# Summing four scan directions in PSUM: the add to y moves from VectorE to TensorE and ScalarE

## The chip, the core and the metric

The kernel runs on one core of a Trainium2 chip. The metric is the time of one execution on the device in microseconds (us), the median of several runs. A core has five engines with instruction queues of their own, worked off in order: TensorE (PE in the profile; its weight loads are PEld), VectorE (DVE), ScalarE (ACT), GpSimd (POOL) and SyncE (SP), which here issues all DMA transfers. The engines wait for each other through semaphores. Products of TensorE land in PSUM, eight banks of 128 x 512 float32; everything else lives in SBUF or in DRAM.

## What is computed

Four images of 96 channels by 64 x 64 pixels pass through four layers. The first is a block with a selective scan over the 4096 pixels in four directions, followed by a gated normalisation and an MLP; the second is a smaller scan block; the third a Fourier block with an 8-bit feed-forward part; the fourth linear attention with such a part. The part that matters here is the scan of the first layer, for 192 channels, 16 states and 4 directions:

```
dt = softplus(einsum('bkrl,kdr->bkdl', dts_r, dt_projs_w) + dt_projs_b)
def step(hst, inp):
    dA  = exp(dt_t[..., None] * A[None])
    dBx = dt_t[..., None] * B_t * x_t[..., None]
    hst = hst * dA + dBx
    y_t = einsum('bkdn,bkn->bkd', hst, C_t)
ys = scan(step, 0, ...) + Ds * xs
ysum = y[:, 0] + undo_colmajor(y[:, 1]) + flipped(y[:, 2]) + undo_colmajor(flipped(y[:, 3]))
```

Directions 0 and 2 run along the rows of the image, forward and backward, directions 1 and 3 along its columns. The output is the sum over all four directions.

## The kernel before

**Stages.** `setup` and the first parts of `front` prepare the first image. Then `scan` runs over all four images; beside it a *stream* of other work (the rest of `front` for all images, the prepared weights, and `rest`, which is everything behind the scan of an image: `tail`, `l1`, `transform`, `middle`, `back`) is put between its instructions. When the scan is over, what is left of the stream runs alone: the end of the last image's `tail`, and its `l1` to `back`.

**The scan** walks 64 chunks: 4 images (batches) x 4 directions (order 0, 1, 3, 2) x 4 steps of 1024 pixels. A chunk has 24 tiles of 128 x 1024: 3 parts p of 64 channels, 4 groups g of states, 2 halves a; a tile holds 32 channels by 4 states. Each tile i goes through:

- `input_of` (L748): GpSimd makes w = u x B. It is issued 3 tiles ahead (`AHEAD`), into one of 9 buffers (`W`).
- `decay` (L144 by way of `act`): ScalarE makes h = exp(dt x A). It is issued two tiles ahead, and there are two buffers, in PSUM.
- the scan itself (L824): VectorE's TENSOR_TENSOR_SCAN over h and w.
- the product with C. Most tiles have it on VectorE (L832); for some GpSimd makes it (L844). `POOL_OUT` says for how many of 24, by image: 5, 8, 8, 8.
- a copy of the last column into `state`, for the next step of the direction: by ScalarE (L840) where VectorE makes the product, by GpSimd (L837) where GpSimd does. The last step of a direction has none.
- `sums` (L770): for each pair of tiles four products by TensorE, 32 columns wide each, add the 4 states of a channel and gather the 8 tiles of a part p in one PSUM bank, `py`. There is one such bank. They are issued three tiles behind the scan.
- `add_sums` (L782 or L785): when the bank holds a part's sums, VectorE adds them to `y`, which lies in SBUF and gathers all directions. In the column directions `y` is read and written with a step of 64 elements (L782), else plainly (L785). It is issued behind the scan of tile i, for a part that ended at tile i - 4. At the last direction the part of `y` then goes to DRAM (`y_ds`), and `y_there` lets the image's `tail` start on it.

**The order of the work** is written when the program is built, by a planner in the kernel. `tick` and `spend` add estimated costs to a clock per engine. After each scan and after each product `advance` compares: how late TensorE, ScalarE and GpSimd stand against VectorE's clock; if that is within a limit (`FIRST` = 2 us behind the scan, `SECOND` = 1 us behind the product), it lets the stream do one step. VectorE's own work for the stream is put off (`later`) until its inputs are estimated to be there (`flush`). `need` steps the stream by force until a chunk's inputs are made. SyncE's queue follows the same order.

```
late = max(chain["pe"] - 0.5, now["act"], now["pool"] - 6.0, now["pe"] - 2.0) - free
if not put_off and late <= slack:
    step()
```

**Constants** lie in SBUF for the whole kernel: `vec` (152 columns, 96 of them A), `negA`, `l1cen` and others. `ident`, a 128 x 128 identity, exists only in `setup`, where `idup` is made from it.

Of the kernel before, what the change touches and what calls it, by code (L numbers as in the profile page):

```python
# [26 lines left out]

DIRS = (0, 1, 3, 2)

POOL_OUT = (5, 8, 8, 8)  # L30

AHEAD, W = 3, 9

LANDED = 8.0

FIRST, SECOND = 2, 1
ENGINES = ("pe", "act", "dve", "pool")

_VECS = [
    ("g1", 1), ("b1", 1), ("bz01", 1), ("bz2", 1), ("cb01", 1), ("cb2", 1),
    ("dtb01", 4), ("dtb2", 4), ("A", 96),
    ("D01", 4), ("D2", 4), ("og01", 1), ("og2", 1), ("ob01", 1), ("ob2", 1), ("opb", 1), ("g2", 1), ("b2", 1),
    ("mb1", 3), ("mb2", 1),
    ("l1cb", 1), ("l1dtb", 2), ("l1A", 2), ("l1D", 2), ("l1og", 1), ("l1ob", 1), ("l1sc", 1),
# [10 lines left out]
def tile_hybrid(ctx: ExitStack, tc: tile.TileContext, I: dict, out: bass.AP):  # L57
# [65 lines left out]
    def right(name, bufs=1):  # L123
        return sb(name, bufs, "right")
# [7 lines left out]
    def act(o, i, func, own=False, **kw):  # L132

        if func in (AF.Exp, AF.Ln):
            if table[0] != "ln exp":
                nc.scalar.preload_act_table_set("natural_log_exp_and_others")  # L136
            table[0] = "ln exp"
        elif func in (AF.Silu, AF.Gelu, AF.Softplus):
            if table[0] != func:
                spend("act", 2.6)  # L140
            table[0] = func
        if not own:
            spend("act", 0.25 + size(o) * 0.86e-3, (i,), (o,))
        nc.scalar.activation(o, i, func, **kw)  # L144
# [76 lines left out]
    def cvec(shape, name):  # L221
        return const.tile(shape, F32, name=name)
# [10 lines left out]

    eps = cvec([128, 1], "eps")
    dve.memset(eps, EPS)

    idup = cvec([128, 32], "idup")
    cen = cvec([C, C], "cen")
# [3 lines left out]
    wz = cvec([C, DI], "wz")  # L242
    fold = cvec([128, 5], "fold")
    negA = cvec([128, 96], "negA")
    l1A = cvec([128, 2], "l1A")
    dsum = cvec([128, 3], "dsum")
    m1 = cvec([C, 384], "m1")
    l1cen = cvec([C, C], "l1cen")
    bn2 = cvec([C, 2], "bn2")
    wc_d = dram.tile([C + 1, 9, DI], F32, name="wc_d")  # L250
    l1wc_d = dram.tile([C, 9, C], F32, name="l1wc_d")
# [7 lines left out]
    def setup():  # L259

        held, (wk,) = pools(sb("set"))
        ident = wk.tile([128, 128], F32, name="ident")

        wraw = wk.tile([C, DI], F32, name="wraw")
        dma(wraw, I["w_inT"][:, 0:DI])
        bi = wk.tile([C + 1, DI], F32, name="bi")
        dma(bi[C : C + 1], I["bi"])
        cwr = wk.tile([C + 1, 9, DI], F32, name="cwr")
        dma(cwr, I["cwT"].partition_broadcast(C + 1))
        wx = wk.tile([C + 1, DI], F32, name="wx")  # L270
        pool.tensor_scalar(wx[rC], wraw, V("g1", rC), None, ALU.mult)
        pf = bank("pf")
        mm(pf[C : C + 1, 0:DI], lhsT=V("b1", rC), rhs=wraw, start=True, stop=True)
        dve.tensor_add(wx[C : C + 1], pf[C : C + 1, 0:DI], bi[C : C + 1])

        act(negA, V("A", n=96), AF.Exp)
        act(l1A, V("l1A", n=2), AF.Exp)
        dve.tensor_scalar_mul(negA, negA, -1.0)
        dve.tensor_scalar_mul(l1A, l1A, -1.0)
        dve.reduce_sum(dsum[:, 0:1], V("D01", n=4), axis=mybir.AxisListType.X)  # L280
        dve.reduce_sum(dsum[:, 1:2], V("D2", n=4), axis=mybir.AxisListType.X)
        dve.reduce_sum(dsum[rC, 2:3], V("l1D", rC, n=2), axis=mybir.AxisListType.X)

        def filters(wc):


            pool.tensor_mul(wc, wx[:, None, :].to_broadcast([C + 1, 9, DI]), cwr)
            dma(wc_d, wc)
            make_identity(nc, ident)
            dve.reduce_sum(idup, ident.rearrange("p (c n) -> p c n", n=4), axis=mybir.AxisListType.X)  # L290

        return held, filters

    def weights():
# [8 lines left out]
        def task():  # L303
# [32 lines left out]
            l1wc = wk.tile([C, 9, C], F32, name="l1wc")  # L336
            pool.tensor_mul(l1wc, w1raw[:, None, :].to_broadcast([C, 9, C]), l1cwr)
            dma(l1wc_d, l1wc)
            pool.tensor_scalar(l1cen, cen, dsum[rC, 2:3], None, ALU.mult)
            l1w = wk.tile([C, 2, C], F32, name="l1w")  # L340
            pw = bank("pw")
            for k in range(2):
# [315 lines left out]
    def scan(pls, advance, need, last_pass):  # L658
# [92 lines left out]
        def sums(i):  # L751

            ci, p, g, a = tiles[i]
            if a == 0:
                return
            if g == 0:
                py[ci, p] = ps.tile([128, 512], F32, tag="py", name="py")
            col = chunks[ci][1] % 2
            flags = dict(start=(g == 0), stop=(g == 3))
            for h in range(2):  # L760
                for e in range(2):
                    q = 32 * (2 * h + e)
                    o = py[ci, p][q : q + 32]
                    v = ws[i - 1 + e]
                    if col:
                        v = v.rearrange("p (w a q r) -> p q w a r", w=16, a=4, q=2)[:, h]
                        o = o.rearrange("p (w a r) -> p w a r", w=16, a=4)
                    else:
                        v = v[:, 512 * h : 512 * h + 512]
                    nc.tensor.matmul(o, lhsT=idup, rhs=v, **flags)  # L770
            t_sum[i - 1] = t_sum[i] = tick("pe", 1.5, t_out[i - 1], t_out[i])

        def add_sums(ci, p):
            b, k, step = chunks[ci]
            lo = start(ci)
            t = y[b][p]
            s = py.pop((ci, p))
            tick("dve", 0.7)
            if k % 2:
                w = lo // HH  # L780
                v = t.rearrange("p (a r w) -> p w a r", a=4, w=WW)[:, w : w + 16]
                dve.tensor_add(v, v, s.rearrange("p (w a r) -> p w a r", w=16, a=4))  # L782
            else:
                v = t[:, lo // 2 : lo // 2 + 512]
                dve.tensor_add(v, v, s)  # L785
                if k == DIRS[-1]:
                    for h, r in enumerate((lo64, hi64)):
                        dma(y_ds[b][64 * p : 64 * p + 64, lo + 512 * h : lo + 512 * h + 512], v[r])
                    if p == 2:
                        y_there.update((b, lo // 512 + h) for h in range(2))  # L790
# [14 lines left out]
        for i, (ci, p, g, a) in enumerate(tiles):  # L805
            b, k, step = chunks[ci]
            x = i % 24
            loads(ci, x)
            if x == 0:
                if step == 0:  # L810
                    states[b, k] = ck.tile([128, 24], F32, tag="state", name="state")
                if step == 0 and k == DIRS[-1]:
                    last_pass(b)
            if i >= 3:
                sums(i - 3)
            input_of(i + AHEAD)

            h, w = hs.pop(i), ws[i]
            pool_out = (x * POOL_OUT[b]) % 24 < POOL_OUT[b]
            o = w if pool_out else h  # L820
            r = slice(None, None, -1) if k >= 2 else slice(None)
            j = 4 * (2 * p + a) + g
            state = states[b, k][:, j : j + 1]
            dve.tensor_tensor_scan(o[:, r], h[:, r], w[:, r], state if step else 0.0, ALU.mult, ALU.add)  # L824
            t_out[i] = tick("dve", 2.35, t_h.pop(i), t_w.pop(i))
            if i >= 4 and tiles[i - 4][2:] == (3, 1):
                add_sums(*tiles[i - 4][0:2])
            flush(now["dve"])
            advance(now["dve"] + (0.0 if pool_out else 1.2), FIRST)
            cc = ccs[ci, g]  # L830
            if not pool_out:
                dve.tensor_mul(w, o, cc)  # L832
                t_out[i] = tick("dve", 1.23)
            if step < NCH - 1:
                last = 0 if k >= 2 else CH - 1
                if pool_out:
                    pool.tensor_copy(state, o[:, last : last + 1])  # L837
                    tick("pool", 0.19, t_out[i])
                else:
                    nc.scalar.copy(state, o[:, last : last + 1])  # L840
                    tick("act", 0.16, t_out[i])
            decay(i + 2)
            if pool_out:
                pool.tensor_mul(w, o, cc)  # L844
# [6 lines left out]
        add_sums(len(chunks) - 1, 2)  # L851

# [139 lines left out]
    def l1(b, stats, xa):  # L992
# [101 lines left out]
        yield from run([conv(m) for m in range(4)], n)  # L1094
        st2.close()

        st3, (ld, wk) = pools(right("l1m", two_groups(n)), right("l1n", n))
        carry = {}

        def states(k, m, order, w):  # L1100
# [528 lines left out]
def _layout(a):  # L1629
# [14 lines left out]
    db = p["dt_projs_b"].T  # L1644
    put("dtb01", db[0:128]); put("dtb2", db[128:192], both)

    put("A", p["A_logs"].reshape(4, 6, 32, 4, 4).transpose(2, 4, 0, 1, 3).reshape(128, 96))
# [22 lines left out]
    for e, rows in enumerate(((0, 6, 38), (32, 64, 80))):  # L1670
# [9 lines left out]
    wo = np.stack([wo[0:128], np.concatenate([wo[128:], wo[128:]])], axis=1)  # L1680
    wqkv = np.concatenate([np.asarray(a["L3_attn_Wqkv"]), np.asarray(a["L3_attn_bqkv"])[None]])
    d = dict(
        vec=vec, x=np.asarray(a["x"]).reshape(B, C, L),
        w_inT=p["in_proj_w"].T, bi=bi[None, 0:DI], cwT=p["conv_w"].reshape(DI, 9).T, xw=xw, dtw=dtw,
        out_projT=wo, mlp1T=p["mlp_w1"].T,
        mlp2T=p["mlp_w2"].T.reshape(3, 128, C).transpose(1, 0, 2),
# [30 lines left out]
```

## Time and profile before

| what | us |
|---|---|
| median of 3 runs | 6782.12 |
| lowest and highest run | 6772.63, 6800.76 |
| profiled execution | 6794.76 |
| its span | 6793.0 |
| first and last start of the scan (L824) | 97.9 and 6218.7 |
| granted TensorE clock, mean over the span | 0.746 |

The span begins with the first instruction and ends with the last; the profiled execution is 1.8 us longer than its span. A line of groups gives the source line, engine, operation, output <- inputs, shapes and count, then the busy time in us and the mean duration of one in ns, then the engine's idle time in front of these instructions and what ended most of it. A line of waits gives who waited <- for whom, the sum in us, how many times, and the longest. A line of windows gives a stretch, its length, and the busy time of each engine in it with the number of instructions, then the granted clock of TensorE (1 is full speed), the busy share of the DMA engines and GB/s. One float32 product of TensorE appears as two MATMUL records.

### The profile page before, as it was taken

Reading aid. Unit: us, or ns where it says so; the run is one execution under the profiler, and the core shown is the slowest. Engines: PE = TensorE matmul, PEld = TensorE weight load, DVE = VectorE, ACT = ScalarE, POOL = GpSimd, SP = SyncE. Lnnn points to the kernel's source line nnn. Section 1 sums busy time; section 2 is a strip of 40 time slices with the busy share of each in tenths; the row PEclk is TensorE's granted clock in tenths of the full one; section 3 lists DMA queues with packets and bytes.
Section 4 is the critical chain, followed back from the end, with each engine's and each line's share of the span. In section 5 each row is a group of like instructions: output and inputs, shape, how many; then the busy total and the mean of one; then the engine's idle time right before and its main releaser. Section 6 shows DMA issues by size and latency. Waiting matters only on the chain. (4 is left out here: it accounts for less than half of the span.)

```text
span 6793.0 us, 52666 instructions
## 1 busy us (share of the span) xinstructions
PE 4648.9 (68%) x15538; PEld 1509.5 (22%) x15538; DVE 5625.5 (83%) x3920; ACT 3691.3 (54%) x5194; POOL 5189.1 (76%) x2732
## 2 busy tenths in 40 slices
PE   6758667677677566656766676657676665567878
PEld 2112112121112124211111132211121242111354
DVE  3888779797789999998899998898899989985324
ACT  3556546565555554565555545565555455664335
POOL 4888879899769888898688788897797889983000
PEclk8767677686677778766777787668787777677887
DMA  4766666667534347445443365345443474442141
GB/s 147 212 193 192 190 180 198 194 208 223 166 109 151 114 132 259 149 130 160 145 147 111 122 225 184 126 142 154 142 134 122 146 250 136 140 153 91 43 113 50
DMA packets 502464, 1049.99 MB, mean 155 GB/s; under 512 B 138449, under 2 KB 252179, under 8 KB 501145
## 3 DMA queue, kind: packets, MB, share of 16 engines
q1 hardware_dynamic: 502176, 1046.63, 49.8%
q8 instruction: 123, 2.02, 0.1%
q14 instruction: 165, 1.34, 0.1%
HBM read 831.15 MB, written 211.09 MB: 153 GB/s over the span
## 5 line engine op out<-in xcount | busy, mean ns | idle before, releaser
L748 POOL TENSOR_TENSOR w<-u,bb 128x1024 f32<-128x1024 f32 x1536 | 3588.8, 2360 | 169.9 <-PE py L770 110.9
L144 ACT ACTIVATE h<-dt,negA 128x1024 f32<-128x1024 f32 x1536 | 1706.6, 1117 | 795.8 <-DVE w L832 429.3
L824 DVE TENSOR_TENSOR_SCAN h<-h,state,w 128x1024 f32<-128x1024 f32 x804 | 1887.0, 2347 | 271.4 <-ACT h L144 201.2
L832 DVE TENSOR_TENSOR w<-h,cc 128x1024 f32<-128x1024 f32 x1072 | 1308.9, 1221 | 56.0 <-DMA cc<-bc_d 18.1
L770 PE MATMUL py<-w,idup 128*32 128x512 f32 x6144 | 1121.1, 802 | 246.6 <-POOL w L844 78.2
L844 POOL TENSOR_TENSOR w<-w,cc 128x1024 f32<-128x1024 f32 x464 | 1092.2, 2354 | 191.6 <-DVE w L824 161.5
L824 DVE TENSOR_TENSOR_SCAN w<-h,state,w 128x1024 f32<-128x1024 f32 x348 | 814.5, 2340 | 46.1 <-ACT h L144 28.7
L840 ACT COPY state<-h 128x1 f32<-128x1 f32 x804 | 127.5, 159 | 1279.8 <-DVE w L832 1279.0
L824 DVE TENSOR_TENSOR_SCAN h<-h,w 128x1024 f32<-128x1024 f32 x268 | 612.9, 2287 | 100.7 <-ACT h L144 69.0
L98 PE MATMUL pc<-xp 97*64 97x512 f32 (+1 forms) x1152 | 401.3, 612 | 12.6 <-DMA xp<-wc_d 7.2
L770 PEld LDWEIGHTS py<-w,idup 128*32 128x32 f32 x6144 | 164.4, 126 | 1059.1 <-issue 605.7
L837 POOL COPY state<-w 128x1 f32<-128x1 f32 x348 | 64.5, 185 | 360.6 <-DVE w L824 353.1
L111 POOL TENSOR_TENSOR u<-dt,xi 128x512 f32<-128x512 f32 x160 | 217.3, 1376 | 158.6 <-ACT dt L144 147.9
L824 DVE TENSOR_TENSOR_SCAN w<-h,w 128x1024 f32<-128x1024 f32 x116 | 264.3, 2279 | 72.2 <-ACT h L144 55.0
L98 PE MATMUL pc<-xp,wc 96*96 96x512 f32 x576 | 275.1, 631 | 25.6 <-ACT u L144 25.6
L98 PE MATMUL pd<-xd,dtw 6*64 6x512 f32 (+1 forms) x512 | 210.9, 979 | 92.3 <-ACT xd L148 57.9
L98 PE MATMUL pcen<-t,cen 96*96 96x512 f32 x192 | 139.3, 866 | 158.9 <-POOL t L1341 77.0
L144 ACT ACT_TABLE_LOAD x176 | 225.8, 1283 | 31.9 <-PE pd L98 18.2
L136 ACT ACT_TABLE_LOAD x174 | 223.2, 1283 | 3.8 <-PEq L1707 0.7
L98 PEld LDWEIGHTS pc<-xp 97*64 97x64 f32 (+1 forms) x1152 | 150.6, 168 | 270.8 <-issue 235.4
L98 PE MATMUL po<-hq,q 128*96 128x512 fp8e5 x192 | 86.7, 575 | 167.0 <-POOL hq L1326 132.0
L98 PE MATMUL px<-xi,xw 128*96 128x512 f32 (+1 forms) x192 | 140.4, 990 | 87.3 <-ACT xi L144 82.4
(245 smaller groups left out, 6309.6 us busy)
## 6 DMA issues: line engine op xcount, KB each, us to landing
u<-u_d SPq DMA_DIRECT2D x384, 512.0 KB
dt<-dt_d SPq DMA_DIRECT2D x384, 512.0 KB
bb<-bc_d SPq DMA_DIRECT2D x256, 512.0 KB
cc<-bc_d SPq DMA_DIRECT2D x256, 512.0 KB
dt_d<-dt SPq DMA_DIRECT2D x128, 256.0 KB
u_d<-u SPq DMA_DIRECT2D x128, 256.0 KB
f_d<-fo SPq DMA_DIRECT2D x64, 384.0 KB
a<-f_d SPq DMA_DIRECT2D x64, 384.0 KB
```

Source lines behind the costliest of these rows:

```text
L98: nc.tensor.matmul(o, lhsT=lhsT, rhs=rhs, **kw)
L111: aside(0.2 + size(o) * 2.1e-3, o, a, b).tensor_mul(o, a, b)
L136: nc.scalar.preload_act_table_set("natural_log_exp_and_others")
L144: nc.scalar.activation(o, i, func, **kw)
L748: pool.tensor_mul(w, us[ci, 2 * p + a], bbs[ci, g])
L770: nc.tensor.matmul(o, lhsT=idup, rhs=v, **flags)
L824: dve.tensor_tensor_scan(o[:, r], h[:, r], w[:, r], state if step else 0.0, ALU.mult, ALU.add)
L832: dve.tensor_mul(w, o, cc)
L837: pool.tensor_copy(state, o[:, last : last + 1])
L840: nc.scalar.copy(state, o[:, last : last + 1])
L844: pool.tensor_mul(w, o, cc)
```

## The change

The add to `y` becomes part of the sums: as the last product of a part, TensorE multiplies the old `y` by the identity, into the same bank (`of_sums` gives the bank and the piece of `y` in one layout). ScalarE then copies the bank to `y` (`keep_sums`). The copy is issued behind the decay of tile i + 2, where the add stood behind the scan of tile i. The planner is told 0.7 us more of TensorE, 0.65 us of ScalarE, and no longer 0.7 us of VectorE.

`POOL_OUT` becomes 4, 7, 7, 7, and the limits `FIRST` and `SECOND` become 3 and 1.5 us.

To make room, `ident` becomes a constant, A is loaded straight into `negA` and leaves `vec`, and `l1cen` goes to DRAM in `weights` and is loaded in `l1` for each image, at the start of the pools of its scans.

```diff
-POOL_OUT = (5, 8, 8, 8)
+POOL_OUT = (4, 7, 7, 7)
...
-FIRST, SECOND = 2, 1
+FIRST, SECOND = 3, 1.5
...
+    ident = cvec([128, 128], "ident")
...
+    dma(negA, I["A"])
...
-        act(negA, V("A", n=96), AF.Exp)
+        act(negA, negA, AF.Exp)
...
+            l1cen = wk.tile([C, C], F32, name="l1cen")
             pool.tensor_scalar(l1cen, cen, dsum[rC, 2:3], None, ALU.mult)
+            dma(l1cen_d, l1cen)
...
-            flags = dict(start=(g == 0), stop=(g == 3))
+            flags = dict(start=(g == 0), stop=False)
...
-            t_sum[i - 1] = t_sum[i] = tick("pe", 1.5, t_out[i - 1], t_out[i])
+            if g == 3:
+                o, v = of_sums(ci, p)
+                nc.tensor.matmul(o, lhsT=ident, rhs=v, start=False, stop=True)
+            t_sum[i - 1] = t_sum[i] = tick("pe", 1.5 + 0.7 * (g == 3), t_out[i - 1], t_out[i])
...
-        def add_sums(ci, p):
+        def of_sums(ci, p):
             b, k, step = chunks[ci]
             lo = start(ci)
-            t = y[b][p]
-            s = py.pop((ci, p))
-            tick("dve", 0.7)
+            t, o = y[b][p], py[ci, p]
             if k % 2:
                 w = lo // HH
                 v = t.rearrange("p (a r w) -> p w a r", a=4, w=WW)[:, w : w + 16]
-                dve.tensor_add(v, v, s.rearrange("p (w a r) -> p w a r", w=16, a=4))
-            else:
-                v = t[:, lo // 2 : lo // 2 + 512]
-                dve.tensor_add(v, v, s)
+                return o.rearrange("p (w a r) -> p w a r", w=16, a=4), v
+            return o, t[:, lo // 2 : lo // 2 + 512]
+
+        def keep_sums(ci, p):
+            b, k, step = chunks[ci]
+            lo = start(ci)
+            o, v = of_sums(ci, p)
+            py.pop((ci, p))
+            tick("act", 0.65, t_sum[24 * ci + 8 * p + 7])
+            nc.scalar.copy(v, o)
+            if k % 2 == 0:
                 if k == DIRS[-1]:
...
-            if i >= 4 and tiles[i - 4][2:] == (3, 1):
-                add_sums(*tiles[i - 4][0:2])
             flush(now["dve"])
...
             decay(i + 2)
+            if i >= 4 and tiles[i - 4][2:] == (3, 1):
+                keep_sums(*tiles[i - 4][0:2])
...
-        st3, (ld, wk) = pools(right("l1m", two_groups(n)), right("l1n", n))
+        st3, (wp2, ld, wk) = pools(right("l1c"), right("l1m", two_groups(n)), right("l1n", n))
+        l1cen = wp2.tile([C, C], F32, name="l1cen")
+        dma(l1cen, l1cen_d)
```

More of the change, by code (lines that the diff above doesn't have):

```diff
@@ L42 @@
     ("g1", 1), ("b1", 1), ("bz01", 1), ("bz2", 1), ("cb01", 1), ("cb2", 1),
-    ("dtb01", 4), ("dtb2", 4), ("A", 96),
+    ("dtb01", 4), ("dtb2", 4),
     ("D01", 4), ("D2", 4), ("og01", 1), ("og2", 1), ("ob01", 1), ("ob2", 1), ("opb", 1), ("g2", 1), ("b2", 1),
@@ L247, in tile_hybrid @@
     m1 = cvec([C, 384], "m1")
-    l1cen = cvec([C, C], "l1cen")
+    l1cen_d = dram.tile([C, C], F32, name="l1cen_d")
     bn2 = cvec([C, 2], "bn2")
@@ L261, in setup @@
         held, (wk,) = pools(sb("set"))
-        ident = wk.tile([128, 128], F32, name="ident")
         wraw = wk.tile([C, DI], F32, name="wraw")
@@ L850, in scan @@
             sums(len(tiles) + i)
-        add_sums(len(chunks) - 1, 2)
+        keep_sums(len(chunks) - 1, 2)
     x1_ds, t_ds = {}, {}
@@ L1645, in _layout @@
     put("dtb01", db[0:128]); put("dtb2", db[128:192], both)
-    put("A", p["A_logs"].reshape(4, 6, 32, 4, 4).transpose(2, 4, 0, 1, 3).reshape(128, 96))
+    A = p["A_logs"].reshape(4, 6, 32, 4, 4).transpose(2, 4, 0, 1, 3).reshape(128, 96)
     put("D01", p["Ds"].T[0:128]); put("D2", p["Ds"].T[128:192], both)
@@ L1682, in _layout @@
     d = dict(
-        vec=vec, x=np.asarray(a["x"]).reshape(B, C, L),
+        vec=vec, A=A, x=np.asarray(a["x"]).reshape(B, C, L),
         w_inT=p["in_proj_w"].T, bi=bi[None, 0:DI], cwT=p["conv_w"].reshape(DI, 9).T, xw=xw, dtw=dtw,
```

## The prediction, made before the changed kernel ran

> **What bounds the kernel now.** I read the page's busy line first, then busy time by window, then the waits of VectorE (DVE), ScalarE (ACT) and GpSimd (POOL), then the groups that the change touches. The lists of line L824 put the first scan at 97.9 us; VectorE ends its last scan-stage instruction, the add at L785, at 6224.3 us. So the span has three parts: 98 us of preparation, 6126 us of scan stage, 569 us after it.
>
> The page's busy line and costliest groups (count, then busy us and mean ns of one, then idle before):
>
> ```profile
> PE 4648.9 (68%) x15538; PEld 1509.5 (22%) x15538; DVE 5625.5 (83%) x3920; ACT 3691.3 (54%) x5194; POOL 5189.1 (76%) x2732
> ...
> L748 POOL TENSOR_TENSOR w<-u,bb 128x1024 f32<-128x1024 f32 x1536 | 3588.8, 2360 | 169.9 <-PE py L770 110.9
> L144 ACT ACTIVATE h<-dt,negA 128x1024 f32<-128x1024 f32 x1536 | 1706.6, 1117 | 795.8 <-DVE w L832 429.3
> ...
> L832 DVE TENSOR_TENSOR w<-h,cc 128x1024 f32<-128x1024 f32 x1072 | 1308.9, 1221 | 56.0 <-DMA cc<-bc_d 18.1
> ...
> L844 POOL TENSOR_TENSOR w<-w,cc 128x1024 f32<-128x1024 f32 x464 | 1092.2, 2354 | 191.6 <-DVE w L824 161.5
> ...
> L840 ACT COPY state<-h 128x1 f32<-128x1 f32 x804 | 127.5, 159 | 1279.8 <-DVE w L832 1279.0
> ```
>
> A product with C costs 1.22 us on VectorE and 2.35 on GpSimd, and ScalarE stands idle 1279 us before its small state copies, waiting for VectorE. Busy time in the scan stage alone (window, length, then PE, PEld, DVE, ACT, POOL), and in one late stretch:
>
> ```profile
> 98.00:6224.00 6126.00, 4162.01 (x13804) 1271.41 (x13804) 5433.70 (x3620) 3441.26 (x4762) 5171.66 (x2705) 0.74 0.52 162
> ...
> 2778.00:3161.00 383.00, 222.87 (x780) 65.64 (x779) 362.63 (x235) 242.03 (x349) 372.22 (x197) 0.71 0.45 145
> ```
>
> VectorE is busy 89% of the stage, GpSimd 84%, ScalarE 56%, TensorE 68% at a mean granted clock of 0.74. In most stretches VectorE is fullest; in the second one GpSimd is (97%). So the stage is VectorE's 5434 us plus 692 us of its idle time. What that idle time waited for (us, times, longest), from VectorE's waits in that window:
>
> ```profile
> DVE h L824 <- ACT h L144: 270.2, 140, 13.6
> DVE w L824 <- ACT h L144: 83.7, 16, 51.7
> DVE y L782 <- PE py L770: 68.0, 26, 6.7
> DVE y L785 <- PE py L770: 64.8, 16, 16.0
> DVE h L824 <- POOL w L748: 51.0, 38, 3.0
> DVE h L824 <- ACT state L840: 44.1, 25, 7.2
> ```
>
> The 51.7 us is the start, outside the stage. Left are 302 us for ScalarE's decay h, 133 us in which an add of the sums waited for TensorE, 56 us for GpSimd's w (5 of them at another row), 73 us for states.
>
> **The change, part by part.** Counts are from the built programs' instruction order.
>
> *Adds leave VectorE.* 192 adds go, 96 of each form:
>
> ```profile
> L782 DVE TENSOR_TENSOR y<-y,py 128x512 f32<-128x512 f32 x96 | 114.9, 1197 | 68.1 <-PE py L770 68.0
> L785 DVE TENSOR_TENSOR y<-y,py 128x512 f32<-128x512 f32 x96 | 64.6, 673 | 64.8 <-PE py L770 64.8
> ```
>
> That is 179.5 us busy. In the timeline an instruction starts some 0.08 us before the end of the one in front, so 164 us comes off the path: **-164**.
>
> *Products come to VectorE.* GpSimd took 5, 8, 8, 8 of 24 per chunk, now 4, 7, 7, 7: 64 products over 64 chunks. Start to start one costs 1.14 us: **+73**.
>
> *The wait for the sums moves.* The 133 us at the adds, in 42 waits, leave VectorE; ScalarE's copy has them now. It stands in ScalarE's queue behind the decay of tile i+2, so it is asked for one product (1.2 us) and one decay (1.1) later than the add was, and what follows it, a state copy that itself waits for VectorE's next product, is needed some 2.3 us after that; the identity product in front takes 1.2 of this back. Net 3.4 us of cover. In the timeline 39 of the 133 us lie beyond the first 3.4 us of their wait, so **-94**; the bounds are -133 and 0. Queued behind the waiting copy are the stream's activations, the next state copies and the next decay, for which the scan waits.
>
> *ScalarE's load.* The trace has no copy by ScalarE out of py; the nearest are its 128x512 copies from other PSUM banks, ca from pca at 0.58 us and yb from pcb at 0.61. 192 at 0.58 are 111 us, and 48 more state copies at 0.16 are 8: 56% busy becomes about 60%. It lies beside VectorE wherever ScalarE waits (the 1279 us); it costs where the decay is already late, which was so at 155 of 1536 scans, a tenth. So 12 us at the least, 119 if each delayed a scan. I take **+35**, nearer the low end, because the late tenth comes in bunches where the copies are late too. For the column directions (96 of the copies) the destination steps by 256 bytes; the VectorE add with those steps took 1.197 us where the plain one took 0.673. [...] No row here shows ScalarE writing so.
>
> *TensorE's load.* 192 identity products, 128 rows by 128 columns by 512. The nearest row, avg in the gated stage, took 39.6 us for 64 records, two to a product: 1.24 us each, 238 us together, 68% busy becomes 74%. It isn't the fullest engine, but the sums are made in its queue. It already waits for the add before it may write the bank again:
>
> ```profile
> 2027.56 0.67 DVE L785 TENSOR_TENSOR y<-y,py 128x512 f32<-128x512 f32 x1
> ...
> 2028.29 3.89 PE L770 MATMUL py<-w,idup 128*32 128x512 f32 x16 [6.21 <-DVE y L785]
> ```
>
> In the stage this cost it 144 us. With the copy 2.3 us later than the add, all that stands behind it (next sums, the stream's products) is held longer, and the w buffers come free later: GpSimd waits 111 us for them today. Nine buffers against three tiles ahead leave about two tiles, 7 us. It gets only work and holds, so no gain; at the most a tenth of them, as with the late decays, reaches VectorE: (238 + 192 x 2.3) / 10 = 68. **+20**, nearer 0, for the buffers.
>
> *GpSimd's load* falls by 64 x 2.354 + 48 x 0.185 = 160 us. VectorE waited 56 us for it, and in stretches like the second window it was the limit. Bounds 0 and -56; **-15**.
>
> *Wider limits* (2 to 3, 1 to 1.5 us of estimated lateness) let the stream be stepped sooner. In the built order the stream stands 0.5 to 2 chunks earlier: the tail of batch 1 starts in chunk 30.7, not 31.8. Behind the scan stage stands the same last tail task and the same rest, so the 569 us stay. With the old limits in the changed program the last tail would start in chunk 63.7, and more would be left behind. The tail of batch 2 now stands one task to a chunk, where two shared one (4590 to 4707 us, TensorE busy 88 of 117). VectorE is idle 77 us in the three such windows of the later batches; half of it is the gain's bound. Against that, a later ScalarE is accepted: 140 late decays by up to 1 us. Bounds -40 and +140; **-10**: the old lateness was paid in a tenth of the scans, the spreading is seen in the order.
>
> *Setup*: one more transfer for A, a smaller vec, l1cen through memory (one store, four loads, each hidden by the forward scan in front of its use): under 2 us, 0 taken.
>
> **Sum**: -164 + 73 - 94 + 35 + 20 - 15 - 10 = -155. The profiled execution took 6794.8 us (span 6793.0), 12.6 above the median of the runs, 6782.1. So 6640 on the profile's footing, **6627 us** on the median's.
>
> **Rivals.**
>
> *A: the freed time isn't used.* Up to 2012 us VectorE is busy 78 to 88% by the windows and waits for the stream (front parts, table loads). If the chains there, and in the tails, set the pace, the adds' time turns into more waiting for h. A third of the adds and all of the moved wait lost: -109 + 73 + 35 + 20 - 15 - 10 = -6, so with the rest of the terms within their bounds 6700 to 6800. For it: VectorE's idle time clusters there. Against it: the adds' waits were VectorE's own.
>
> *B: slower, by ScalarE's queue.* A copy whose sums are late stops every decay behind it, and two decays ahead is all the scan has. Price: the 133 us stay; the copies land on a late ScalarE at 0.6 us, 119 in all; later steps add 140 x 1 us. -164 + 73 + 119 + 140 = +168 without any other gain, 6950; the middle of it about 6860. It decides from the point where the added lateness is over the 91 us by which adds exceed products: about 150 copies of 192 paid in full. Against it: only a tenth of the scans found the decay late.
>
> *C: more than the sum.* VectorE and GpSimd both get shorter, so stretches that alternate between them lose both: all 133 of the wait, 56 of GpSimd's, 40 by spread tails, ScalarE at 12: -164 + 73 - 133 + 12 - 56 - 40 = -308, 6474; the middle about 6520.
>
> *D: it doesn't do what it says.* The built order has the adds gone, 1136 products on VectorE and 400 on GpSimd, so no.
>
> **Chances.** Forecast (6560 to 6700) 0.50; C 0.20; A (6700 to 6815) 0.18; B 0.12. Range 6520 to 6770: it leaves out half of C, a bit of A and B. About 0.5% (34 us) is what a measurement can tell from no change: faster 0.77, same 0.11, slower 0.12.
>
> **What would show it.** Right: scan stage near 5970 us; VectorE about 5340 busy in it; no VectorE wait for py; ScalarE's copy of y at 0.6 us, its waits for py under 60 us; VectorE's wait for h under 350; the part behind the stage at 569. Wrong: h waits above 430 (B), a copy in the column directions over 1 us, GpSimd waiting over 200 us for py, or the part behind the stage longer by a tail task.

## The result, and the profile after

The changed kernel takes 6878.8 us (median; 6878.06 to 6882.23), the kernel before 6782.1 beside it: a ratio of 1.0108, interval 1.0079 to 1.0136. It is slower, by 73 us; the prediction was 6627. TensorE's granted clock, 0.758 in the profiled execution for 0.746 before, isn't lower. The profiled execution has a span of 6880.4 us. In the page's busy line and groups the lines have moved: the scan is L837, the product with C L843, the sums L773; the identity product is L777 and ScalarE's copy L797.

```profile
PE 4871.1 (71%) x15922; PEld 1574.9 (23%) x15922; DVE 5547.5 (81%) x3792; ACT 3842.0 (56%) x5434; POOL 5038.4 (73%) x2620
...
L144 ACT ACTIVATE h<-dt,negA 128x1024 f32<-128x1024 f32 x1536 | 1712.2, 1118 | 640.2 <-DVE w L843 406.4
L843 DVE TENSOR_TENSOR w<-h,cc 128x1024 f32<-128x1024 f32 x1136 | 1388.4, 1222 | 79.2 <-DMA cc<-bc_d 2.5
L773 PE MATMUL py<-w,idup 128*32 128x512 f32 x6144 | 1097.7, 799 | 487.5 <-ACT y L797 353.3
...
L777 PE MATMUL py<-y,ident 128*128 128x512 f32 x384 | 325.7, 937 | 15.4 <-DMA y<-yin_d 15.4
```

VectorE has 78 us less to do (5547.5 for 5625.5) and GpSimd 151 us less, as the change intends; TensorE has 222 us more, and it stood idle 353 us before the sums for ScalarE's copy, where it had waited 144 for the adds. By window (length, then PE, PEld, DVE, ACT, POOL), the scan stage and the part behind it:

```profile
98.00:6297.00 6199.00, 4372.01 (x14180) 1334.34 (x14180) 5354.22 (x3491) 3590.07 (x5001) 5021.48 (x2594) 0.75 0.52 160
6297.00:6880.00 583.00, 455.13 (x1625) 225.07 (x1624) 189.33 (x290) 228.08 (x397) 1.56 (x8) 0.80 0.27 78
```

The stage before, cut by the same measure:

```profile
98.00:6221.00 6123.00, 4159.57 (x13793) 1271.05 (x13797) 5430.77 (x3616) 3441.26 (x4762) 5171.66 (x2705) 0.74 0.52 162
```

Here and below the stage runs from the start of the first scan to the end of the last. Before it was 6123 us with 572 behind it; it is now 6199 with 583, although VectorE is busy 77 us less in it. So VectorE stands idle longer. Its waits (us, times, longest; the 51.2 is the start, outside the stage):

```profile
DVE h L837 <- ACT h L144: 358.3, 153, 15.9
DVE h L837 <- ACT state L851: 151.0, 68, 15.4
DVE w L837 <- ACT h L144: 94.0, 23, 51.2
DVE w L837 <- ACT state L851: 59.9, 15, 9.8
...
DVE h L837 <- POOL w L751: 24.6, 14, 7.7
```

No row for `py` is left: the 133 us of waiting for the sums are gone. But in front of the scans VectorE now waits 612 us for ScalarE (the four rows together without the start), where it waited 375. One of these waits, in ScalarE's timeline (start, duration, then in brackets the idle time in front) and then VectorE's:

```profile
4554.01 1.12 ACT L144 ACTIVATE h<-dt,negA 128x1024 f32<-128x1024 f32 x1
4555.07 0.58 ACT L797 COPY y<-py 128x512 f32<-128x512 f32 x1
4555.66 1.28 ACT L144 ACT_TABLE_LOAD   x1
4561.84 0.69 ACT L144 ACTIVATE za<-pz,fold 128x512 f32<-128x512 f32 x1 [4.89 <-PE pz L98]
4563.55 0.69 ACT L144 ACTIVATE za<-pz,fold 128x512 f32<-128x512 f32 x1 [1.02 <-PE pz L98]
4565.46 0.69 ACT L144 ACTIVATE zb<-pz,fold 128x512 f32<-128x512 f32 x1 [1.23 <-PE pz L98]
4566.04 0.15 ACT L851 COPY state<-h 128x1 f32<-128x1 f32 x1
4566.21 1.28 ACT L136 ACT_TABLE_LOAD   x1
4567.51 1.12 ACT L144 ACTIVATE h<-dt,negA 128x1024 f32<-128x1024 f32 x1
```

```profile
4557.30 2.34 DVE L837 TENSOR_TENSOR_SCAN w<-h,state,w 128x1024 f32<-128x1024 f32 x1
4568.73 2.36 DVE L837 TENSOR_TENSOR_SCAN h<-h,state,w 128x1024 f32<-128x1024 f32 x1 [9.09 <-ACT h L144]
```

Between two decays stand, beside the copy of `y` and a state, three activations of the tail with their table loads. These take 4.6 us of the 12.4 between the decays; 7.1 is idle time in which ScalarE waits for TensorE's `pz`. TensorE itself had stood idle for 13.44 us, at the end for a transfer, `xh`, before it began these products at 4559.76. So the decay behind them is late by more than ScalarE's load would tell. Added over all rows, ScalarE waited for TensorE 548 us in the stage before and 691 in the stage after.

### The profile page after: what moved, and what is told of

It reads as the page before. It is cut to its first block, busy times and chain, and to the rows that moved or that the text cites. A ratio compares the mean times of both kernels' runs of the same rounds, so it can differ in the third digit from the quotient of the medians.

```text
span 6880.4 us, 54043 instructions
## 1 busy us (share of the span) xinstructions
PE 4871.1 (71%) x15922; PEld 1574.9 (23%) x15922; DVE 5547.5 (81%) x3792; ACT 3842.0 (56%) x5434; POOL 5038.4 (73%) x2620
## 5 line engine op out<-in xcount | busy, mean ns | idle before, releaser
L751 POOL TENSOR_TENSOR w<-u,bb 128x1024 f32<-128x1024 f32 x1536 | 3589.0, 2361 | 265.3 <-PE py L773 224.5
L837 DVE TENSOR_TENSOR_SCAN h<-h,state,w 128x1024 f32<-128x1024 f32 x852 | 1999.3, 2347 | 401.7 <-ACT h L144 273.5
L843 DVE TENSOR_TENSOR w<-h,cc 128x1024 f32<-128x1024 f32 x1136 | 1388.4, 1222 | 79.2 <-DMA cc<-bc_d 2.5
L773 PE MATMUL py<-w,idup 128*32 128x512 f32 x6144 | 1097.7, 799 | 487.5 <-ACT y L797 353.3
L857 POOL TENSOR_TENSOR w<-w,cc 128x1024 f32<-128x1024 f32 x400 | 942.3, 2356 | 183.1 <-DVE w L837 154.6
L837 DVE TENSOR_TENSOR_SCAN w<-h,state,w 128x1024 f32<-128x1024 f32 x300 | 702.2, 2341 | 80.1 <-ACT state L851 48.7
L837 DVE TENSOR_TENSOR_SCAN h<-h,w 128x1024 f32<-128x1024 f32 x284 | 649.4, 2287 | 141.6 <-ACT h L144 84.8
L773 PEld LDWEIGHTS py<-w,idup 128*32 128x32 f32 x6144 | 156.3, 125 | 1258.5 <-issue 605.0
L98 PE MATMUL pc<-xp 97*64 97x512 f32 (+1 forms) x1152 | 419.4, 639 | 7.7 <-ACT dt L144 7.7
L777 PE MATMUL py<-y,ident 128*128 128x512 f32 x384 | 325.7, 937 | 15.4 <-DMA y<-yin_d 15.4
L837 DVE TENSOR_TENSOR_SCAN w<-h,w 128x1024 f32<-128x1024 f32 x100 | 228.1, 2281 | 79.6 <-ACT h L144 68.4
L144 ACT ACTIVATE dt<-pd,vec 128x512 f32<-128x512 f32 (+1 forms) x256 | 162.8, 684 | 66.2 <-DMA dt_d<-dt 54.3
```

Of the source, the lines that this page charges most:

```text
L98: nc.tensor.matmul(o, lhsT=lhsT, rhs=rhs, **kw)
L751: pool.tensor_mul(w, us[ci, 2 * p + a], bbs[ci, g])
L777: nc.tensor.matmul(o, lhsT=ident, rhs=v, start=False, stop=True)
```

## The experiments

In all of them "limits" are `FIRST, SECOND`; waits are VectorE's for ScalarE's decays and states in front of the scans, in the stage. Stage, behind and waits come from one profiled execution of each run, the time in us is the median of all. Ratios are to the kernel before on the same chip; where I take the difference of two ratios, its uncertainty is the root of the sum of the squares of both half-widths, times 6805 us, the median of before in those runs.

| run | limits | POOL_OUT | sums | us | ratio [interval] | stage | behind | waits |
|---|---|---|---|---|---|---|---|---|
| before | 2, 1 | 5 8 8 8 | add | 6782.1 | 1 | 6123 | 572 | 375 |
| after | 3, 1.5 | 4 7 7 7 | moved | 6878.8 | 1.0108 [1.0079, 1.0136] | 6199 | 583 | 612 |
| e1 | 2, 1 | 4 7 7 7 | moved | 6823.5 | 1.0033 [1.0011, 1.0054] | 6045 | 675 | 462 |
| e2 | 3, 1.5 | 5 8 8 8 | add | 6909.8 | 1.0156 [1.0127, 1.0186] | 6222 | 572 | 495 |
| e3 | 2, 1 | 4 7 7 7 | add | 6866.4 | 1.0095 [1.0065, 1.0126] | 6203 | 581 | 352 |
| e4 | 3, 1.5 | 5 8 8 8 | moved | 6896.6 | 1.0140 [1.0112, 1.0168] | 6209 | 582 | 667 |
| e5 | 3, 1 | 4 7 7 7 | moved | 6876.5 | 1.0093 [1.0073, 1.0112] | 6191 | 583 | 585 |
| e6 | 2.5, 1 | 4 7 7 7 | moved | 6811.2 | 1.0004 [0.9990, 1.0019] | 6143 | 563 | 569 |
| e7 | 2, 1, from the third image 3, 1.5 | 4 7 7 7 | moved | 6843.9 | 1.0046 [1.0029, 1.0062] | 6153 | 591 | 549 |
| e8 | 3, 1.5 | 4 7 7 7 | VectorE copies | 6990.8 | 1.0280 [1.0235, 1.0326] | 6311 | 573 | 475 |
| e9 | 5, 3, both behind the decay | 4 7 7 7 | moved | 6835.0 | 1.0044 [1.0025, 1.0063] | 6118 | 605 | 523 |
| e10 | 2, 2.5 | 4 7 7 7 | moved | 6809.0 | 1.0011 [0.9990, 1.0033] | 6159 | 574 | 560 |
| e11 | 1.5, 3 | 4 7 7 7 | moved | 6803.2 | 0.9987 [0.9973, 1.0000] | 6132 | 582 | 561 |
| e12 | 2, 1, from the second image 1.5, 3.5 | 4 7 7 7 | moved | 6800.3 | 0.9991 [0.9974, 1.0008] | 6117 | 569 | 521 |
| e13 | 2, 1, from the second image 6, 4 behind the decay | 4 7 7 7 | moved | 6841.7 | 1.0051 [1.0031, 1.0070] | 6120 | 606 | 546 |
| e14 | 3, 1.5 | 4 7 7 7 | no copy | 6833.6 | 1.0043 [1.0027, 1.0060] | 6156 | 566 | 587 |
| e15 | 3, 1.5 | 4 7 7 7 | no copy, no identity product | 6817.8 | 1.0015 [1.0000, 1.0029] | 6153 | 565 | 600 |
| e16 | 2, 1 | 4 7 7 7 | no copy, no identity product | 6737.3 | 0.9905 [0.9881, 0.9929] | 5964 | 675 | 392 |
| e17 | 2, 1, planner told the old costs | 4 7 7 7 | moved | 6809.1 | 1.0005 [0.9989, 1.0020] | 6132 | 584 | 534 |
| e18 | 2, 1, planner told nothing of the sums | 4 7 7 7 | moved | 6803.9 | 0.9993 [0.9973, 1.0013] | 6081 | 607 | 488 |

Two theories stood at the start. In *Theory L* the wider limits are what costs: steps of the stream that are let through late stand in front of a decay. In *Theory Q* it is the moved sums: copies in ScalarE's queue, and the bank they hold.

### The parts alone (e1 to e4)

e1 is the changed kernel with the old limits, e2 the kernel before with the wide ones; e3 is the kernel before with the new `POOL_OUT`, e4 the changed one with the old.

```diff
e1  -FIRST, SECOND = 3, 1.5        +FIRST, SECOND = 2, 1
e2  -FIRST, SECOND = 2, 1          +FIRST, SECOND = 3, 1.5
e3  -POOL_OUT = (5, 8, 8, 8)       +POOL_OUT = (4, 7, 7, 7)
e4  -POOL_OUT = (4, 7, 7, 7)       +POOL_OUT = (5, 8, 8, 8)
```

> The changed kernel with the limits of before (2 and 1 us); everything else as changed. In the built order the stream then stands later, and three tail tasks of the last image are left behind the scan stage instead of one. Theory L (the wider limits let the stream's activations in ahead of the decays, and that is what makes VectorE wait for ScalarE): the scan stage falls from 6205 us to about 5980, VectorE's waits for ScalarE (h and state together) from 612 back to about 400 us; with some 120 us of tail work more behind the stage the total is about 6680. Theory Q (the copies themselves, standing in ScalarE's queue and holding the only bank of the sums, are what costs): the scan stage stays within 40 us of 6205, waits for ScalarE stay above 550, total 6900 to 7000.

> The kernel before with the wider limits alone (3 and 1.5 us). In the built order as much is left behind the scan stage as before. Theory L: slower by about as much as the changed kernel's added waits, 6860 to 6930, VectorE's waits for ScalarE up from 375 to 500 or more. Theory Q: within 30 us of before, 6750 to 6810, waits for ScalarE near 375.

> The kernel before with 4, 7, 7, 7 products on GpSimd alone: 64 products more on VectorE. If VectorE's own work sets the pace of the scan stage (as the prediction's sum had it): 73 us slower, about 6850. If its waits set the pace and work put on it only fills idle time: within 25 us of before, 6760 to 6805. If GpSimd was the tighter one: faster by up to 56 us, 6730.

> The changed kernel with 5, 8, 8, 8 products on GpSimd as before: 64 products fewer on VectorE. If VectorE's own work sets the pace: 73 us faster than the changed kernel, about 6806. If its waits for ScalarE set the pace: within 25 us of the changed kernel, 6855 to 6905.

Alone, the wide limits make the kernel before 106 us slower (86 to 127), more than the whole change (33 us more than after, 5 to 61). VectorE's waits in e2 rise to 495 us while those for the sums stay:

```profile
DVE h L824 <- ACT h L144: 327.6, 135, 13.5
DVE w L824 <- ACT h L144: 77.5, 12, 51.5
DVE w L824 <- ACT state L840: 73.6, 21, 13.1
DVE y L782 <- PE py L770: 72.8, 29, 6.9
DVE h L824 <- ACT state L840: 68.2, 36, 13.1
DVE y L785 <- PE py L770: 63.3, 23, 11.7
```

One thing goes along with it. e2's stage by window has the work of before, but TensorE takes 57 us more for it (4217 for 4160):

```profile
98.00:6320.00 6222.00, 4217.47 (x13798) 1274.01 (x13798) 5441.44 (x3618) 3445.71 (x4762) 5171.48 (x2705) 0.72 0.51 160
```

Over whole executions the granted clock was 0.732 in e2 (mean of four) and 0.745 in the kernel before beside it. Among the 114 executions of the kernel before that were timed beside the experiments, the time is some 46 us longer for a clock lower by 0.01; by that slope, an estimate, up to 60 of the 106 us could come with the clock. Whether the lower clock is a cause of the longer time or comes of it, no run shows.

In the changed kernel they cost less, 51 us (27 to 75, after against e1), because there they also buy something. By window, e1's stage and what is behind it:

```profile
99.00:6144.00 6045.00, 4255.10 (x13962) 1301.92 (x13962) 5331.20 (x3446) 3521.94 (x4908) 5015.47 (x2593) 0.76 0.53 164
6144.00:6818.00 674.00, 554.14 (x1843) 255.63 (x1842) 221.77 (x335) 281.56 (x480) 1.56 (x8) 0.85 0.25 71
```

With the old limits the stage is 78 us shorter than before, but the last image's tail starts in chunk 63.7 and not 61.8, since the planner is told more of TensorE and ScalarE, and 103 us more is left behind the stage. The wide limits take 92 of these away (583 for 675) and lengthen the stage by 154. So Theory L holds for what happens in the stage, but e1 is no gain either: something else is missing. (The 6680 that Theory L gave for e1 was also added up wrongly: 98 of preparation, 5980 of stage, 583 and 120 behind it are 6781.) The products alone (e3) cost 65 us (44 to 86); undone in the changed kernel (e4) they bring nothing back, 22 us slower and not outside the uncertainty of 27.

### How wide, and where (e5 to e7, e9 to e13)

The edits of e7, e12 and e13 are given in words.

```diff
e5   +FIRST, SECOND = 3, 1          e6   +FIRST, SECOND = 2.5, 1
e10  +FIRST, SECOND = 2, 2.5        e11  +FIRST, SECOND = 1.5, 3
e7   +FIRST, SECOND = 2, 1 in images 0 and 1; 3, 1.5 in images 2 and 3
e12  +FIRST, SECOND = 2, 1 in image 0; 1.5, 3.5 in the others
e9   +FIRST, SECOND = 5, 3
     -            advance(now["dve"] + (0.0 if pool_out else 1.2), FIRST)
...
                  decay(i + 2)
     +            advance(now["dve"], FIRST)
e13  as e9 from the second image on, with 6, 4; the first as in e1
```

> The changed kernel with 3 us behind the scan and the old 1 us behind the product. What the first limit lets in stands in front of the next decay in ScalarE's queue, what the second lets in stands behind it. If the first limit is what makes decays late: VectorE's waits for ScalarE stay above 570 us (612 in the changed kernel), total 6860 to 6900. If the second is: they fall to about 480, the scan stage to about 6080, and with the same one tail task behind (583 us) the total is about 6760. If both share: about 6820.

> The changed kernel with 2.5 and 1 us. If the wait for ScalarE grows evenly with the limits: between the old limits (462 us of waits, stage 6045) and the wide ones (612, 6199), so about 520 and 6110. One or two tail tasks are left behind the stage in the built order, 583 to 640 us. Total 6800 to 6840. If only the last step from 2.5 to 3 costs: stage about 6060, total 6750.

> The changed kernel with the old limits for images 0 and 1 and the wide ones for images 2 and 3. If the price of the wide limits (154 us in the stage for four images) spreads over the images: stage about 6045 + 77 = 6120, with two tail tasks behind 625, total about 6845. If it is paid where many front parts are made, in image 0 alone: stage about 6050, total about 6775, less than before.

`FIRST` alone carries the price: with 3 and 1 the time is that of the changed kernel, with 2.5 and 1 it is back at before's. e7 lies between e1 and after: the two later images pay for their wide limits too (1550 and 1548 us of stage, against 1472 and 1515 in e1).

My arithmetic for this was a cover: the decay of tile i + 2 is wanted one scan and one product (3.6 us) after the product of tile i and takes 1.1, so stream work let through in front of it has some 2.4 us from the product's end; 2 lies below that and 3 above. A step behind the product has 3.6. From this came Theory C.

> The changed kernel with the stream's step behind the scan moved behind the decay of tile i + 2, and limits 5 and 3 there (both now stand behind the decay; in the built order the last tail begins in chunk 62.7, between the 61.2 of the changed kernel and the 63.7 of the one with the old limits). Theory C (cover): what costs is stream work on ScalarE in front of a decay that has only 2.4 us of cover from the end of the product, so out of its way VectorE's waits for ScalarE are at most the 462 us of the changed kernel with the old limits, the stage is near 6040, the part behind it 620 to 650, the time 6760 to 6800. Theory E (early): stream work costs wherever it is brought forward, by the same as with wider limits: waits about 600, stage 6190, time above 6880.

> The changed kernel with the limits 2 and 2.5: the old one behind the scan, a wide one behind the product. The last tail begins in chunk 61.3, as in the changed kernel (61.2). Theory C: the step behind the product has 3.6 us of cover, so 2.5 stays within it: waits for ScalarE 460 to 500 us, stage 6045 + 23 for two more tail tasks = about 6070, behind 585, time about 6750. Theory E: as the changed kernel, waits 600, stage 6190, time 6870.

> The changed kernel with the limits 1.5 and 3: tighter than the old one behind the scan, wider still behind the product; the last tail begins in chunk 61.2. Theory C: 3 is still within the 3.6 us of cover, and fewer steps stand in front of the decay: waits for ScalarE 430 to 480 us, stage about 6050, behind 583, time about 6730. Theory E: waits 600, stage 6190, time 6870.

Half of it held. The stream stands in the same place as after (the last tail starts in chunk 61.3 and 61.2, after in 61.2), but bought behind the product it costs 66 to 82 us less: e10 and e11 are 0.0097 and 0.0121 below after in ratio. So the step in front of the decay is the dear one. e9 came out between the two theories, with 523 us of waits and a stage of 6118. But the gains forecast, to 6750 and 6730, didn't come: the stage is 87 to 114 us longer than e1's, about what the shorter part behind gives. In e11 and e9 the first image had by far the most of the waits (221 and 210 us, against 121 in e1; no later image more than 121), hence the next two.

> The changed kernel with the old limits (2, 1) in the first image and (1.5, 3.5) in the others; the last tail begins in chunk 61.8, as in the kernel before. Theory F (the remainder is the first image's): the first image as with the old limits throughout, 1521 us, the others as in the run with 1.5 and 3, 1520 + 1515 + 1497, so a stage of 6053, 590 behind it, time about 6740. Theory E (it is paid wherever the stream is early): the first image's gain is given back by the others, stage 6120 to 6140, time about 6800.

> The changed kernel with the old limits and places in the first image, and in the others both steps behind the decay with limits 6 and 4; the last tail begins in chunk 62.8, so about 35 us more than before is left behind the stage. Theory F: first image 1521, the others as in the run with both steps behind the decay, 1490 + 1505 + 1499, so a stage of 6015 to 6035, 620 behind it, time about 6750. Theory E: stage 6110 or more, time above 6820.

Theory F fell. The first image came as forecast, 1519 us in both, but the second, 1520 and 1490 in e11 and e9, came at 1555 and 1562: what the first image no longer paid, the second did. e11 and e12 tie with before; with e18 below (0.9987 to 0.9993) they are the best versions with the moved sums.

### The place without the limits (e17, e18)

The planner can also be led to the same place of the stream by what it is told of the sums, with the limits at 2 and 1. In e17 it is told what it was told before, in e18 nothing.

```diff
-            t_sum[i - 1] = t_sum[i] = tick("pe", 1.5 + 0.7 * (g == 3), t_out[i - 1], t_out[i])
+            t_sum[i - 1] = t_sum[i] = tick("pe", 1.5, t_out[i - 1], t_out[i])
...
-            tick("act", 0.65, t_sum[24 * ci + 8 * p + 7])
+            tick("dve", 0.7)        (e17; in e18 the line is gone)
```

> The changed kernel with the old limits 2 and 1, the planner told of the sums what it was told before (0.7 us of VectorE, nothing for the identity product and the copy); the last tail begins in chunk 61.2, as in the changed kernel. If the late steps are what costs (Theory L): stage 6045 + 23 = about 6070, behind 575, time about 6745. If the earlier position has the price itself (Theory E): stage 6130 to 6190, time 6805 to 6870.

> The changed kernel with the old limits, the planner told nothing of the sums; the last tail begins in chunk 63.0, between the 63.7 of the changed kernel with the old limits and the 61.8 of the kernel before. Theory L: stage about 6060, behind 620 to 640, time about 6790. Theory E: stage 6080 to 6100, behind the same, time about 6820.

e17's stage by window:

```profile
98.00:6231.00 6133.00, 4316.12 (x14180) 1316.52 (x14180) 5359.91 (x3492) 3585.64 (x5001) 5019.49 (x2594) 0.76 0.52 162
```

The same instructions as after in another order (PE, ACT and DVE counts agree but for one of DVE), the last tail at the same 61.2, and yet 67 us less of stage: that is the price of the late steps. It includes whatever comes with the clock: TensorE is busy 56 us less for the same products (4316 for 4372), at a mean clock of 0.766 over all executions for after's 0.759. And 87 us more than e1: that is the price of the earlier stream itself, two tail tasks more in the stage, which give back 91 behind it. Put side by side, stage and rest behind it come to 6686 to 6733 us in e1, e6, e10 to e12, e17 and e18, and to 6695 before: wherever the stream stood, with limits up to 2.5 in front of the decay, the profiles gave one time within 0.7%.

### What the moved sums cost by themselves (e8, e14 to e16)

e8 keeps the identity product and lets VectorE copy the bank, in the add's old place. e14 leaves out ScalarE's copies, e15 and e16 leave out the identity products as well, so the directions aren't summed there; the planner is told the same costs, and the order of the rest is the same.

```diff
e8   -            nc.scalar.copy(v, o)
     +            dve.tensor_copy(v, o)        (behind the scan, VectorE told 0.7)
e14  -            nc.scalar.copy(v, o)
e15  as e14, and
     -                nc.tensor.matmul(o, lhsT=ident, rhs=v, start=False, stop=True)
     -            flags = dict(start=(g == 0), stop=False)
     +            flags = dict(start=(g == 0), stop=(g == 3))
e16  as e15, and  +FIRST, SECOND = 2, 1
```

> The changed kernel, but VectorE copies the bank of the sums to y, at the place where the add stood; ScalarE has no copies and the planner charges VectorE 0.7 us in their stead. If the 192 copies in ScalarE's queue add their part to the late decays: VectorE's waits for ScalarE fall from 612 to about 500 (495 with the wide limits alone), its waits for TensorE at the copy come back with 100 to 180 us, its busy time grows by 110 to 180; total 6880 to 6960. If the copies are harmless and TensorE's identity products and holds are the cost: waits for ScalarE stay above 580 and the total goes over 6980.

> The changed kernel without ScalarE's 192 copies of the bank to y; the sums over directions are left out of the output, the order of everything else is the same. My sum: the copies cost 35 us, so about 6845. Theory P (the price of the copies is what was freed): they hold ScalarE 154 us (192 at 0.80) and it waits 34 us in front of them, nearly all of it seen by the scan, so 6700 to 6730, VectorE's waits for ScalarE near 450. Theory A (the freed time isn't used, whoever makes the sums): less than 35 us, waits stay near 600.

> The same, and without the 192 identity products on TensorE (326 us busy in the changed kernel). My sum: another 20 us, so 6825. Theory P: GpSimd's waits for TensorE fall from 226 to about 110 us, another 20 to 60 us of time, so 6650 to 6700. Theory A: 6840 or more.

> The same with the old limits 2 and 1, to be held against the changed kernel with the old limits (6823). My sum: 55 us less, 6770. Theory P: VectorE's waits for ScalarE fall from 462 to about 330, the stage from 6045 to about 5900, time 6660 to 6690. Theory A: stage 6020 or more, time 6790 to 6820.

e8 is 117 us (80 to 154) slower than after: VectorE waits 217 us for `py` again. Of the two engines, ScalarE is the better one for the copy.

e14 and e15 weigh it: after against e14, the copies cost 44 us (22 to 67), e14 against e15, the identity products 19 (4 to 34); both together 87 (65 to 109) with the old limits (e1 against e16). That is my sum's size, 55, or somewhat more, and far less than Theory P asked for. The 19 is a net price: with the identity products gone the granted clock is lower, 0.740 for 0.762. In e15, free of everything that the moved sums put on ScalarE and TensorE, VectorE still waits as long for the decays (the scan is one line higher here):

```profile
DVE h L836 <- ACT h L144: 353.4, 146, 16.9
DVE h L836 <- ACT state L850: 153.7, 68, 15.2
DVE w L836 <- ACT h L144: 95.8, 14, 51.9
DVE w L836 <- ACT state L850: 48.5, 13, 9.6
```

Its stage by window:

```profile
98.00:6251.00 6153.00, 4208.75 (x13798) 1279.25 (x13798) 5368.59 (x3491) 3449.27 (x4810) 5014.65 (x2594) 0.73 0.52 161
```

The waits are 600 us without the start, where e2, with the same limits and the adds, has 495. From e2 to e15 VectorE loses 73 us of work in the stage and 135 of waits for `py`, 208 together, and the stage gets 69 shorter; 105 came back in these rows. That is Theory A: half of the freed time turns into another wait. With the old limits the waits rise less, from 375 to 392 us, but more is left behind the stage. e16's two windows:

```profile
98.00:6063.00 5965.00, 4047.90 (x13580) 1239.64 (x13580) 5327.14 (x3447) 3382.31 (x4718) 5012.34 (x2594) 0.74 0.53 166
6063.00:6737.00 674.00, 558.63 (x1841) 255.99 (x1840) 221.09 (x334) 281.11 (x479) 1.56 (x8) 0.83 0.25 71
```

The stage is 159 us shorter than before and 103 more is left behind. By the 87 us that the two tail tasks cost inside the stage (e17 against e1), some 72 of the 159 would be left with the stream in its place of before, an estimate. Free sums over directions would bring 65 us (48 to 81) all told; the moved sums cost 87.

## Why the prediction was wrong

From before to after by way of e16 and e1: the gains -65, the copies and identity products +87, the wide limits +51; together +73, which is the result. The sum had -200 (adds, products, the wait, GpSimd), +55 and -10. So of the 228 us between the forecast of -155 and the result, 135 lie in the gains, 61 in the limits and 32 in the copies and identity products. Two steps failed.

- **The larger: the gains, -200, taken as time off the stage because VectorE no longer works or waits there.** Its parts hold by themselves. The waits for `py` are gone (133 us, predicted 94 net), and ScalarE waits 34 us for the sums, as against the 39 that I left it. Products and GpSimd's relief, +58, measured +65 (e3). An add took less of the path than I said: counted in the trace of before, where an add stands alone between scan and product (91 of 192), a plain one moves the product by 0.44 us and one with steps by 0.93, so 132 us for all and not 164. But the gains together came to 65 us (e16). With the wide limits, 208 us less of work and waits made the stage 69 shorter, and 105 came back as waits for ScalarE (e2 to e15): the scan can't start earlier than its decay, and with the adds gone the decays are what it finds late. Rival A said this and priced it at 6700 to 6815; e11, e12 and e18, the best versions with the moved sums, lie there, at 0.9987 to 0.9993 of before. The changed kernel itself lies above it, by the limits.
- **The other: "Wider limits ... -10: the old lateness was paid in a tenth of the scans, the spreading is seen in the order."** It measured +51 in the changed kernel and +106 alone. I took a late step to cost at most 1 us, in 140 cases, and to land where the old ones did. A step let through in front of the decay can bring activations that wait for TensorE: the example above cost 9.09 us at once. There TensorE waited for a transfer, but that isn't the rule: its waits for transfers in the stage are 242 us before, 266 after and 193 in e2. The bound of +140 was in the text; the value was taken from the wrong end.
- **"Behind the scan stage stands the same last tail task and the same rest, so the 569 us stay": right** (583, against 572 by the same measure), and right that the old limits would leave more, 103 us. The first scan starts at 98.5 us for 97.9, so nothing was lost in front of the stage either; what the loads of `l1cen` cost by themselves, no run isolates. What I missed is that this isn't a gain: the two tail tasks cost 87 us inside the stage (e1 to e17) for 91 behind it.
- **ScalarE's load, +35: about right.** The copies cost 44 us (22 to 67) for 154.6 us busy, 43.6 more than the 111 of the forecast. In the column directions a copy takes 1.04 us (below), over the 1 us that was named as a sign, and not the 0.58 of the nearest row of before; with a tenth of those 43.6 this term would have been 39 in place of 35.
- **TensorE's load, +20: right** in the price, 19 us (4 to 34), not in the work: an identity product took 1.70 us (325.7 / 192), predicted 1.24. GpSimd's waits for the sums, named as a sign at 200 us, came to 224.5. They rise without the moved sums too: for all that TensorE keeps it waiting in the stage, 111 us before, 179 in e2, 212 in e3, 226 after.
- **Rival B** had the result within 20 us (6860 for its middle) by luck: of its three terms the last, the later steps, is what the runs show, and the copies cost 44 of its 119. Late sums that stop the decays behind a copy weren't it: 34 us of ScalarE's waiting, and e14.

Three things stay open. Why VectorE's waits for ScalarE rise when the adds go, even with no copies: that both wait for the same late TensorE is my reading. ScalarE's waits for TensorE fit it in some runs (658 us in e15, 597 in e2, 548 before, 492 in e16) and not in others (709 in e10, which ties with before, and 652 in e8, where VectorE waits 475), and no run takes that wait away. How much of the limits' price comes with the granted clock. And whether the kernel before would gain from another place of its stream wasn't tried.

## What to carry to other kernels

Time taken from the fullest engine counts only until the next operand is late: here 208 us less of VectorE's work and waits made the stage 69 us shorter, and 105 came back as waits for ScalarE (e2 to e15). Before adding it up, look at how late that operand is where the work to be removed stands; if it is late in the same stretches, the work was partly its cover. A planner's limit for late steps is best changed by itself first: here wider limits alone (3 and 1.5 us for 2 and 1) cost the kernel before 106 us, more than the 73 of the whole change. And work pulled forward from behind a stage into it is a gain only if the stage gets longer by less than the rest gets shorter; here it was 87 for 91.

## What the runs showed of the hardware

ScalarE's copy of a bank to `y` has two durations. In a window of a column direction, where it writes every 64th element (min, median, max in ns):

```profile
L797 ACT COPY y<-py x3: 1027/1037/1057, 570.3 to 626.1; 128x512 f32<-128x512 f32 x3
```

and in one of a row direction, where it writes plainly:

```profile
L797 ACT COPY y<-py x4: 577/578/586, 2003.1 to 2083.1; 128x512 f32<-128x512 f32 x4
```

The ratio, 1.79, is that of VectorE's two adds (1197 to 673 ns, 1.78). And between a scan and the product that follows it at once VectorE's gaps summed to 56 us before (772 pairs) and to 99 in e1 (951 pairs); why they are longer where no adds stand between others is not known.
